# A two-layer graph-attention kernel: the last product of layer 1 is moved directly behind its gather, and the rest of a step is put around it

## The chip, the cores and the metric

The kernel runs on one core of a Trainium2 chip. A core has five engines that run side by side and wait for each other through semaphores: TensorE (PE, the matrix products and transposes; its weight loads are listed apart as PEld), VectorE (DVE), ScalarE (ACT), GpSimd (POOL), and SyncE (SP), which here only issues transfers. TensorE writes to PSUM, a small memory[...]; everything that leaves PSUM is read by VectorE or ScalarE. The metric is the device time of one launch in microseconds. All arithmetic that matters here is in float32.

## The reference, cut to what is computed

There are 32 graphs (batches) of 512 nodes with 512 features, one 512x512 adjacency matrix, and two layers. Each layer is a layer norm, a ReLU, and an attention over the graph, added to its input.

```python
# layer 0: 8 heads of 64, masked softmax attention
h = relu(layernorm(x))
q, k, v = h @ Wq + bq, h @ Wk + bk, h @ Wv + bv          # split into heads
scores = q k^T / 8 + (1 - adj) * -1e9
x = x + (softmax(scores) v) @ Wo + bo
# layer 1: one head, additive attention
h = relu(layernorm(x))
hw = h @ W
e = leaky_relu(s1[:, None] + s2[None, :], 0.2) * adj      # s1, s2: hw times two vectors
x = x + elu(softmax(e) @ hw + beta * hw)
```

## The kernel before: the parts that the change touches

The kernel works on several batches at once. In step `b` it does the attention of layer 0 for batch `b` in four units (one for each pair of heads), the product with Wo for batch `b-1`, layer 1 for batch `b-2`, and the norm, transposes and projections k and q for batch `b+1`. A string gives the order of the parts on TensorE. Digits are units, a dot is the denominators of the unit just finished:

```python
        order = {
            0: "0.V1.NH2c.3wK.Q", 1: "0.VUrR1.W2.NH3K.Q", B - 1: "0.VDU1.rRGX2.W3.t", B: "0yrR.zUWDngY",
            B + 1: "DgJY",
        }.get(b, "0.VDU1.GX2.rYNRWH3.KQ")
```

So in the steps 2 to 30: V is the projection to v, D the small product for layer 1's denominators, U the combinations for Wo, G the gather of layer 1 (`at` times `hn`, four tiles), X the combinations of its result gT, r and R load the two pairs of residual rows, Y is the final product of layer 1, N the transposes of the next batch, W the product with Wo, H the combinations of the transposed rows, K and Q the projections.

Each 512x512x512 product is done in seven half-size block products instead of eight. The seven pieces share three PSUM buffers, x, y and qz[...], and take sums and differences of blocks ("combinations") of the one side, which GpSimd forms:

```python
    def seven(name, w, B, tokens, one, two, scale=1.0, more=None):
        ...
        times(x_, A11, "b11", True);  nc.scalar.copy(y_, x_);            yield
        times(qz[:, 0, :], S1, "t1", True); nc.scalar.activation(q_, qz[:, 0, :], AF.Copy, scale=scale)
        if more: more(q_)                                                # yield
        times(y_, S2, "t2", False, onto=True); nc.scalar.copy(z_, y_);   yield   # z_ is qz[:, 1, :]
        times(x_, A12, "b21", False, onto=True); one(0, 0, x_);          yield
        times(z_, S3, "t3", False, onto=True);   two(1, 1, z_, q_);      yield
        times(y_, S4, "b22", False, onto=True);  two(0, 1, y_, q_);      yield
        times(z_, NA22, "t4", False, onto=True); one(1, 0, z_)
```

(Put on fewer lines here; the kernel has one statement on each.) `one` and `two` empty a finished block. For the final product of layer 1 that is the ELU, in turns on ScalarE and VectorE, and then an addition on GpSimd and the store; y is a pool of three buffers:

```python
        def elu(i, k, s):
            y = wtile([P, N], f"y_{b}_{i}_{k}", "y", 3)
            for t in range(2):
                nc.scalar.activation(y[:, ts(t, H)], s[:, ts(t, H)], AF.Exp, scale=r[...])
            nc.vector.tensor_scalar(y, y, 1.0, -1.0, op0=ALU.min, op1=ALU.add)
            for t in range(2):
                nc.vector.scalar_tensor_tensor(y[:, ts(t, H)], s[:, ts(t, H)], r[...], y[:, ts(t, H)],
                                               op0=ALU.mult, op1=ALU.max)
            ... # GpSimd adds the residual rows, SyncE stores
        def two(i, k, p, q):
            s = wtile([P, N], f"yq_{b}_{i}_{k}", "y", 3)
            nc.vector.tensor_tensor(s, p, q, op=ALU.add)
            elu(i, k, s)
```

A unit first multiplies the exponentials of the unit before with v (`values`, into the PSUM buffer po), then makes four score products into the buffers s, x and y, qz, s. VectorE masks each, ScalarE takes the exponential, VectorE sums the four (es):

```python
            for k, tag in enumerate(("s", "xy", "qz", "s")):
                scores(b, j, k, s, tag)
```

The transposes, sixteen for a batch, go through po, qz and s, and ScalarE empties them with the ReLU:

```python
        def second():
            for c, tag in ((2, "po"), (3, "qz")):
                ...
                turned(p, c)
                nc.scalar.activation(h[1][:, c - 2, :], p, AF.Relu)
        def first():
            p = psum.tile([P, 2, N], F32, name=f"pn0_{b}", tag="s")
            ...
            nc.scalar.activation(h[0], p, AF.Relu)
        for part in (second, first) if b else (first, second):
            part()
```

The combinations of gT: X makes them after the whole gather, with the first one in place; a second form, used by the last steps only, takes the first combination from the first two of the four tiles, into a buffer of its own:

```python
        def X():
            old["gB"] = combos(b - 2, "vT", old["g"])
        def G1():
            G((0, 1))
            t1 = first_combo(b - 2, "vT", old["g"][0], nc.gpsimd)
            G((2, 3))
            old["gB"] = other_combos(b - 2, "vT", old["g"], t1)
        def W():
            need("wa")
            fourth(b - 1, "uT", prev["oT"])      # the fourth combination, GpSimd
            run(out_proj(b - 1, prev))
```

Every engine works through its instructions in the order in which the program records them. For work that can stand anywhere on VectorE (sums, reciprocals, norms) the program keeps a rough clock of its own while it is built, and `GAP` is the allowed delay of two kinds of them, the sums and the reciprocals, for the four units; so the tuple only orders VectorE's instructions.

Of the kernel before, what the change touches and what calls it, by code (L numbers as in the profile page):

```python
# [40 lines left out]

A11, A12, NA22, S1, S2, S3, S4 = range(7)

GAP = (12.0, 14.0, 28.0, 24.0)
GAPS = {0: (14.0, 1.0, 4.0, 24.0), 1: (12.0, 12.0, 2.0, 14.0)}
LAST_GAPS = (3.0, 14.0, 12.0, 3.0)

# [16 lines left out]
def kernel(  # L64
# [86 lines left out]
    def wtile(shape, name, tag, bufs, dt=F32):  # L151
        return work.tile(shape, dt, name=name, tag=tag, bufs=bufs)
# [12 lines left out]
    def pe(us):  # L165

        clock["pe"] += us
        till = clock["pe"] + (1.0 if at_ends[0] else 0.4)
        while True:
            due = [i for i, (_, t, _) in enumerate(ends) if t <= till]  # L170
            fits = [
                (by, i) for i, (_, t, cost, _, by) in enumerate(spare)
                if max(clock["dve"], t) + cost <= till
            ]
            if due:
                ends.pop(due[0])[2]()
            elif fits:
                run_spare(min(fits)[1])
            else:
                return  # L180

    def dve(us):

        clock["dve"] = max(clock["dve"], clock["pe"]) + us
# [10 lines left out]
    def need(key):  # L195

        waits = at_ends[0] and key not in ("e", "es") and any(e[0] == key for e in spare + ends)
        run_all(key)
        if waits:
            clock["pe"] = max(clock["pe"], clock["dve"])  # L200
# [165 lines left out]
    def pair(b, name, p, tag, bufs):  # L366
        return wtile([P, 2, N], f"{name}_{b}_{p}", tag, bufs)
# [15 lines left out]
    def first_combo(b, name, pair0, eng):  # L383

        t1 = wtile([P, 2, H], f"{name}1_{b}", "T", 5)
        eng.tensor_tensor(t1, pair0[:, :, H:], pair0[:, :, :H], op=ALU.subtract)
        return t1
# [8 lines left out]
    def fourth(b, name, B):  # L396

        B["t4"] = wtile([P, 2, H], f"{name}4_{b}", "T", 5)
        nc.gpsimd.tensor_tensor(B["t4"], B["t2"], B["b21"], op=ALU.subtract)

    def turn(b, st):

        xs = st["x"]
        need(("x", b))
        h = [pair(b, "hT", i, "hP", 2) for i in range(2)]

        def turned(p, c):
            for t in range(T):
                nc.tensor.transpose(p[:, ts(t, P)], xs[t][:, ts(c, P)], ident)  # L409

        def second():
            for c, tag in ((2, "po"), (3, "qz")):
                p = psum.tile([P, 1 if c == 2 else 2, N], F32, name=f"pn{c}_{b}", tag=tag)[:, 0, :]
# [5 lines that stand above are left out]
            for c in range(2):  # L419
                turned(p[:, c, :], c)  # L420
            nc.scalar.activation(h[0], p, AF.Relu)

        for part in (second, first) if b else (first, second):
            part()
        pe(2.4)
        st["h"] = h

# [94 lines left out]
    def quarter(p):  # L522
        return p.rearrange("p (t f) -> p t f", t=2)

    def proj_v(b, st):
        v = st["v"] = [pair(b, "v", i, "vP", 2) for i in range(2)]

        def one(i, k, p):
            nc.scalar.copy(v[k][:, :, ts(i, H)], quarter(p))

        def two(i, k, p, r):
            nc.vector.tensor_tensor(v[k][:, :, ts(i, H)], quarter(p), quarter(r), op=ALU.add)
            dve(0.75)

        return seven(f"v{b}", wv, st["hT"], True, one, two)
# [7 lines left out]
    def gap(b, j):  # L543
        return (LAST_GAPS if b == B - 1 else GAPS.get(b, GAP))[j]

# [115 lines left out]
    def out_proj(b, st):  # L661
        x1 = st["x1"]
        st["mv"] = wtile([P, T, 2], f"mv1_{b}", "mv1", 2)
        st["s12"] = wtile([P, 2, T], f"s12_{b}", "s12", 2)
        st["hn"] = [None] * T

        def parts(k, i, p):

            n = 2 // len(x1[k])
            for u, r in enumerate(x1[k]):  # L670
                yield r[:, :, ts(i, H)], quarter(p)[:, u * n : (u + 1) * n, :]

        def add(i, k, p):
            for r, p_ in parts(k, i, p):
                nc.vector.scalar_tensor_tensor(r, p_, 1.0 / VS, r, op0=ALU.mult, op1=ALU.add)  # L675
                dve(0.75 if len(x1[k]) == 1 else 0.45)

        def one(i, k, p):
            add(i, k, p)
            if i == 1:  # L680
                norm1(b, st, (0, 1))

        def two(i, k, p, r):
            add(i, k, p)
            if i == 0:
                norm1(b, st, (2, 3))

        def more(q_):
            for i in (1, 0):
                for r, q in parts(1, i, q_):  # L690
                    nc.gpsimd.tensor_tensor(r, r, q, op=ALU.add)

        return seven(f"w{b}", wo, st["oT"], True, one, two, 1.0 / VS, more)
# [168 lines left out]
    def denominators(b, j):  # L862
        done = (b, j - 1) if j else (b - 1, NP - 1)
        if done[0] in states:
            finish(*done, states[done[0]])

    def step(b):

        cur, nxt = states.get(b), states.get(b + 1)
        prev, old = states.get(b - 1), states.get(b - 2)

        def run(pieces):
            for _ in pieces:
                pass

        def V():
            run(proj_v(b, cur))

        def G(cs=range(C)):
            for c in cs:
                gather(b - 2, c, old)

        def y_(g):
            st = states[g]
            st["pieces"] = final(g, st)
            for _ in range(3):
                next(st["pieces"])

            B = st["gB"]
            B["t4"] = B["t2"]
            nc.gpsimd.tensor_tensor(B["t4"], B["t2"], B["b21"], op=ALU.subtract)

        def z_(g):
            run(states[g]["pieces"])

        def Y():
            y_(b - 2)
            z_(b - 2)  # L900
# [11 lines that stand above are left out]
        def turned():  # L912
            turn(b + 1, nxt)
            if b + 2 < B:
                new_state(b + 2)

        def W():
            need("wa")
            fourth(b - 1, "uT", prev["oT"])
            run(out_proj(b - 1, prev))  # L920


        def H_():
            nxt["hT"] = combos(b + 1, "tT", nxt["h"])

        def K():
            fourth(b + 1, "tT", nxt["hT"])
            run(proj_k(b + 1, nxt))

        def U():  # L930
            need("rd")
            if b == B:
                prev["oT"] = other_combos(b - 1, "uT", prev["o"], prev["t1"])
            else:
                prev["oT"] = combos(b - 1, "uT", prev["o"])

        def T1():
            cur["t1"] = first_combo(b, "uT", cur["o"][0], nc.gpsimd)

        parts = {  # L940
            "V": V, "D": lambda: diagonal(b - 2, old), "G": G, "Y": Y, "N": turned, "W": W,
            "y": lambda: y_(b - 3), "z": lambda: z_(b - 3), "X": X, "g": G1,
            "K": K, "U": U, "H": H_, "r": lambda: residual(b - 1, prev, 0, *(("e", 4) if b == B else ())),
            "t": T1, "n": lambda: run_all(("hn", b - 1)), "J": judge,
            "R": lambda: residual(b - 1, prev, 1, *{B: ("e", 4), B - 1: ("x", 4)}.get(b, ())),
            "Q": lambda: run(proj_q(b + 1, nxt)),
            "c": lambda: value_row(ao, bvr), "w": row_constants,
        }
        order = {
            0: "0.V1.NH2c.3wK.Q", 1: "0.VUrR1.W2.NH3K.Q", B - 1: "0.VDU1.rRGX2.W3.t", B: "0yrR.zUWDngY",  # L950
            B + 1: "DgJY",
        }.get(b, "0.VDU1.GX2.rYNRWH3.KQ")
        unit_ = 0
        at_ends[0] = b < 2 or b >= B - 1
        for part in order:
            if part.isdigit():
                unit_ = int(part)
                unit(b, unit_)
            elif part == ".":
                denominators(b, unit_)  # L960
            else:
                parts[part]()
        states.pop(b - 3, None)
# [18 lines left out]
    with tc.manual_schedule(engines=BY_HAND):  # L982
# [9 lines left out]
        y_ = psum.tile([P, N], F32, name="y_first", tag="y")  # L992
# [231 lines left out]
```

## Time and profile before

The median of three runs is 3856.84 us (3854.91 to 3858.11). The profiled execution spans 3855.6 us.

| engine | busy us | share of the span | instructions |
|---|---|---|---|
| TensorE, products | 3622.9 | 94% | 25845 |
| TensorE, weight loads | 2025.5 | 53% | 25846 |
| VectorE | 2830.3 | 73% | 4335 |
| ScalarE | 1477.2 | 38% | 2310 |
| GpSimd | 1291.1 | 33% | 1090 |

The transfers move 120.82 MB at 31 GB/s on average. The mean granted clock of TensorE is 0.971 of full speed. The products are pipelined and their ends are modelled, so a busy TensorE is not one at its peak: where one piece follows the other, the distance from start to start is the time to count, not the duration. A line of the profile may be that of a helper (L53 is `product`), so the names of the tiles tell the parts apart: `x_y`, `qz_y` and `y_y` are the final product of layer 1, those with `_w` the product with Wo, `pg` the gather, `pn` the transposes, `po` the values, `ps` the scores.

### The profile page before, as it was taken

Reading aid. Unit: us, or ns where it says so; the run is one execution under the profiler, and the core shown is the slowest. Engines: PE = TensorE matmul, PEld = TensorE weight load, DVE = VectorE, ACT = ScalarE, POOL = GpSimd, SP = SyncE. Lnnn points to the kernel's source line nnn. Section 1 sums busy time; section 2 is a strip of 40 time slices with the busy share of each in tenths; the row PEclk is TensorE's granted clock in tenths of the full one; section 3 lists DMA queues with packets and bytes.
Section 4 is the critical chain, followed back from the end, with each engine's and each line's share of the span. In section 5 each row is a group of like instructions: output and inputs, shape, how many; then the busy total and the mean of one; then the engine's idle time right before and its main releaser. Section 6 shows DMA issues by size and latency. Waiting matters only on the chain. (4 is left out here: it accounts for less than half of the span.)

```text
span 3855.6 us, 62638 instructions
## 1 busy us (share of the span) xinstructions
PE 3622.9 (94%) x25845; PEld 2025.5 (53%) x25846; DVE 2830.3 (73%) x4335; ACT 1477.2 (38%) x2310; POOL 1291.1 (33%) x1090
## 2 busy tenths in 40 slices
PE   9999999999999999999999999999999999999986
PEld 5555555555554555555555545555455555555543
DVE  7978777787677776777876778767777767787774
ACT  3433343343333333343434334333433333343432
POOL 5432333322343232333223342324332333322341
PEclk9999999999999999999999999999999999999998
DMA  3010111100111001111011110111110111101100
GB/s 124 17 36 4 37 36 36 34 7 33 37 36 33 24 16 36 36 34 36 4 37 36 36 34 9 31 36 36 34 36 4 36 36 36 34 4 37 31 25 26
DMA packets 88035, 120.82 MB, mean 31 GB/s; under 512 B 11904, under 2 KB 49792, under 8 KB 87744
## 3 DMA queue, kind: packets, MB, share of 16 engines
q1 hardware_dynamic: 86160, 114.91, 9.5%
q8 instruction: 205, 3.36, 0.4%
q10 hardware_dynamic: 1376, 1.57, 0.1%
q14 instruction: 86, 0.70, 0.1%
q0 software_dynamic: 208, 0.27, 0.0%
HBM read 83.11 MB, written 33.62 MB: 30 GB/s over the span
## 5 line engine op out<-in xcount | busy, mean ns | idle before, releaser
L634 POOL TENSOR_TENSOR oT<-oT,rd 128x512 f32<-128x512 f32 x128 | 170.4, 1331 | 1622.4 <-ACT rd L633 1622.2
L582 ACT ACTIVATE e<-e 128x1024 f32<-128x1024 f32 x512 | 541.1, 1057 | 192.1 <-DVE e L567 157.7
L567 DVE SCALAR_TENSOR_TENSOR e<-maskT,ps 128x1024 f32<-128x1024 uint8 x384 | 454.7, 1212 | 145.2 <-PE ps L555 145.0
L555 PE MATMUL ps<-qT,kT 64*128 64x512 f32 x2048 | 483.4, 606 | 12.4 <-DVE e L567 12.4
L605 PE MATMUL po<-e,v 128*64 128x512 f32 x2048 | 463.0, 593 | 0.0
L53 PE MATMUL pg<-at,hn 128*64 128x512 f32 x2048 | 448.6, 596 | 4.2 <-DVE dmax L788 2.1
L628 DVE RECIPROCAL rd<-pd 128x256 f32<-128x256 f32 x256 | 434.9, 1729 | 1.2 <-POOL oT L634 1.2
L579 DVE TENSOR_TENSOR es<-es,e 128x1024 f32<-128x1024 f32 x254 | 342.1, 1347 | 16.9 <-ACT e L582 1.1
L555 PEld LDWEIGHTS ps<-qT,kT 64*128 64x128 f32 x2048 | 184.2, 186 | 309.1 <-issue 213.9
L53 PEld LDWEIGHTS pg<-at,hn 128*64 128x64 f32 x2048 | 148.5, 138 | 297.8 <-issue 289.3
L605 PEld LDWEIGHTS po<-e,v 128*64 128x64 f32 x2048 | 157.0, 138 | 235.9 <-issue 226.1
L409 PE MATMUL pn<-ident,x 128*128 128x128 f32 x512 | 106.4, 379 | 162.1 <-DVE y L816 161.7
L824 POOL TENSOR_TENSOR y<-y,x 128x512 f32<-128x512 f32 x124 | 157.2, 1268 | 245.0 <-DVE y L816 204.5
L613 ACT COPY oT<-po 128x512 f32<-128x512 f32 x128 | 73.8, 576 | 397.5 <-PE po L605 397.5
L675 DVE SCALAR_TENSOR_TENSOR x<-x_w,x 128x512 f32<-128x512 f32 x32 | 22.1, 690 | 274.1 <-issue 262.0
L729 DVE CUSTOM_DVE_ANT_0 scr<-hn,wa_r 128x512 f32<-128x512 f32 x256 | 168.0, 712 | 49.0 <-ACT hn L716 49.0
L756 ACT ACTIVATE at<-at 128x512 f32<-128x512 f32 x128 | 80.4, 628 | 274.4 <-DVE at L752 274.4
L633 ACT ACTIVATE rd<-rd 128x512 f32<-128x512 f32 x128 | 80.7, 630 | 272.6 <-DVE rd L628 272.5
L334 POOL TENSOR_TENSOR rs<-rs,mhalf 128x2 f32<-128x2 f32 (+1 forms) x97 | 77.9, 803 | 317.5 <-DVE rs L333 313.9
L409 PEld LDWEIGHTS pn<-ident,x 128*128 128x128 f32 x512 | 87.5, 198 | 181.6 <-issue 180.7
L654 POOL TENSOR_TENSOR x<-x,c_row 128x512 f32<-128x512 f32 x124 | 158.2, 1298 | 52.4 <-DMA x<-in_x_dram 52.4
L814 DVE TENSOR_SCALAR y<-y 128x512 f32<-128x512 f32 x128 | 61.5, 481 | 153.2 <-ACT y L811 153.2
(221 smaller groups left out, 6796.9 us busy)
## 6 DMA issues: line engine op xcount, KB each, us to landing
x<-in_x_dram SPq DMA_DIRECT2D x128, 256.0 KB, 4.7
out_dram<-y SPq DMA_DIRECT2D x128, 256.0 KB, 2.1
x<-in_x_dram SPq DMA_DIRECT2D x63, 512.0 KB, 4.0
s<-row_s SPq DMA_DIRECT2D x32, 256.0 KB, 4.0
adj<-in_adj_dram SPq DMA_DIRECT2D x4, 256.0 KB, 7.0
wk<-in_L_gnn_Wk_dram ACTq DMA_DIRECT2D x3, 256.0 KB, 9.5
wq<-in_L_gnn_Wq_dram SPq DMA_DIRECT2D x3, 256.0 KB, 7.1
wv<-in_L_gnn_Wv_dram SPq DMA_DIRECT2D x3, 256.0 KB, 5.3
```

Of the source, the lines that this page charges most:

```text
L53: nc.tensor.matmul(out[s : s + HD], lhsT[:, s : s + HD], rhs, start=start, stop=stop, skip_group_check=onto)
L409: nc.tensor.transpose(p[:, ts(t, P)], xs[t][:, ts(c, P)], ident)
L555: nc.tensor.matmul(ps[s], st["kT"][j][rows, ts(k, P)], st["qT"][j][rows, :], start=True, stop=True)
L567: nc.vector.scalar_tensor_tensor(e, maskT[:, k, :].unsqueeze(1).to_broadcast([P, 2, N]), NEG, p, op0=ALU.mult, op1=ALU.add)
L579: (nc.gpsimd if early else nc.vector).tensor_tensor(es, one, e, op=ALU.add)
L582: nc.scalar.activation(e, e, AF.Exp)
L605: nc.tensor.matmul(po[s * HD : (s + 1) * HD, :], v[k // 2][:, k % 2, (2 * j + s) * HD : (2 * j + s + 1) * HD], e[k][:, s, :], start=k == 0 ...
L628: nc.vector.reciprocal(rd[:, ts(k, H)], pd[:, ts(k, H)])
L634: nc.gpsimd.tensor_tensor(o, o, rd, op=ALU.mult)
L654: eng.tensor_tensor(r[:, t, :], r[:, t, :], c_row, op=ALU.add)
L729: nc.vector.tensor_tensor_reduce(scr, st["hn"][t], r, 1.0, 0.0, op0=ALU.mult, op1=ALU.add, accum_out=st["s12"][:, g, t : t + 1],)
L824: (nc.vector if b == B - 2 else nc.gpsimd).tensor_tensor(yu, yu, x_[:, :, ts(i, H)], op=ALU.add)
```

## The change

The order of the steps 2 to 30 becomes: final product of layer 1 directly behind its gather (with the first combination from half the gather), then unit 2, then the product with Wo, the transposes, unit 3, k and q. In the new part M the fourth combination for Wo is formed after the third piece, so that it may take the place of the second combination, which is then used up. The transposes go through s first, then po and qz. The tuple `GAP` is set to the new order. No operation on numbers is added or removed. It is meant to put other work between a product and the next use of the PSUM buffers that it leaves full.

```diff
-GAP = (12.0, 14.0, 28.0, 24.0)
+GAP = (13.0, 26.0, 14.0, 24.0)
...
-        for part in (second, first) if b else (first, second):
-            part()
+        first()
+        second()
...
+        def M():
+            pieces = out_proj(b - 1, prev)
+            for _ in range(3):
+                next(pieces)
+            fourth(b - 1, "uT", prev["oT"])
+            run(pieces)
+
...
-            "K": K, ... "X": X, "g": G1,
+            "K": K, ... "X": X, "M": M, "g": G1,
...
-        }.get(b, "0.VDU1.GX2.rYNRWH3.KQ")
+        }.get(b, "0.VDU1.rgY2.RMNH3.KQ")
```

(The table of parts is cut: M is added to it, and nothing else in it changes.)

More of the change, by code (lines that the diff above doesn't have):

```diff
@@ L941, in step @@
             "V": V, "D": lambda: diagonal(b - 2, old), "G": G, "Y": Y, "N": turned, "W": W,
-            "y": lambda: y_(b - 3), "z": lambda: z_(b - 3), "X": X, "g": G1,
+            "y": lambda: y_(b - 3), "z": lambda: z_(b - 3), "X": X, "M": M, "g": G1,
             "K": K, "U": U, "H": H_, "r": lambda: residual(b - 1, prev, 0, *(("e", 4) if b == B else ())),
```

## The prediction, made before the changed kernel ran

> **What bounds the kernel now.** I read the page's first part, then TensorE's list of waits, then one steady step on each engine. The page gives TensorE 3622.9 us of busy time in a span of 3855.6 us (94%), VectorE 73%, ScalarE 38%, GpSimd 33%. The page's chain of the work that ended last covers only the tail (1% of the span), so it is no help here. The waits of TensorE are (engine, line, releaser: total us, times, longest):
>
> ```profile
> PE pn L409 <- DVE y L816: 161.7, 29, 6.5
> PE pe L53 <- DVE as L763: 19.1, 2, 11.7
> PE ps L555 <- DVE e L567: 12.4, 33, 1.7
> PE qz_w L53 <- DVE y L816: 5.5, 1, 5.5
> PE pd L620 <- DVE rd L628: 3.9, 1, 3.9
> ```
>
> One wait stands out: 29 times, once in each of the steps 2 to 30 that the change rewrites, the transposes of the next batch wait 161.7 / 29 = 5.58 us for the end of the ELU of layer 1. The others lie in the first and last steps, except the 0.33 us of the scores in each step. The timeline of TensorE in such a step (start, duration, engine and line, operation):
>
> ```profile
> 1811.06 1.90 PE L53 MATMUL qz_y<-w,vT 128*64 128x256 f32 x16
> 1812.88 0.66 PE L409 MATMUL pn<-ident,x 128*128 128x128 f32 x4
> 1819.05 2.80 PE L409 MATMUL pn<-ident,x 128*128 128x128 f32 x12 [5.51 <-DVE y L816]
> 1821.77 3.47 PE L53 MATMUL x_w<-wo,oT 128*64 128x256 f32 x16
> 1825.07 1.89 PE L53 MATMUL qz_w<-wo,oT 128*64 128x256 f32 x16
> ...
> 1911.62 3.60 PE L605 MATMUL po<-e,v 128*64 128x512 f32 x16
> 1915.15 3.71 PE L555 MATMUL ps<-qT,kT 64*128 64x512 f32 x16
> 1918.78 1.08 PE L620 MATMUL pd<-es,ones 128*64 128x512 f32 x4
> ```
>
> The reader is to see three things. The seventh piece of the final product starts at 1811.06; a piece takes 1.73 us from start to start, so the product is over for TensorE at 1812.79, which I call E below. The second transposed column, which goes into the PSUM buffer qz, cannot start before 1819.05, which is E + 6.26. And a unit of attention (values, four score products, denominators) takes 1919.69 - 1911.62 = 8.07 us, in which the third score product, again into qz, starts 3.53 + 2 x 0.9 = 5.33 us after the unit's start.
>
> The wait costs more than its length. The stretches of clock (stretch, length, busy times of the five engines, granted clock, DMA):
>
> ```profile
> 1815.00:1819.00 4.00, 0.00 (x0) 0.00 (x0) 2.82 (x7) 1.32 (x3) 1.26 (x1) 0.88 0.30 107
> 1819.00:1822.00 3.00, 2.95 (x14) 2.65 (x16) 1.56 (x1) 0.72 (x2) 1.32 (x2) 0.50 0.87 291
> 1822.00:1825.00 3.00, 3.00 (x16) 1.68 (x16) 0.00 (x0) 0.90 (x1) 3.00 (x3) 0.52 1.02 278
> 1825.00:1828.00 3.00, 3.00 (x32) 1.95 (x28) 0.00 (x0) 1.80 (x4) 2.09 (x3) 1.00 0.70 253
> ```
>
> After the idle time the clock is at half for some 6 us, and the twelve transposes take 2.72 us (1819.05 to 1821.77). In the first batch, at full clock and without a wait, sixteen take 1.80 us, as this line shows (1.97 less a tail of 0.17), so twelve would take 1.35:
>
> ```profile
> 14.11 1.97 PE L409 MATMUL pn<-ident,x 128*128 128x128 f32 x16
> ```
>
> That is 1.37 us lost. The first piece of Wo (x_w) loses too: its group is busy for 149.9 us, the like group x_y for 121.5; 28.4 / 29 = 0.98 us in each step. Together 2.35 us.
>
> [...] the waits of 5.5 us are followed by half clock, the one of 3.87 us (near 128 us) too, with 0.57 in the stretch after it, while a wait of 1.69 us at 79 us leaves the clock at 1.00. [...] the three sums es take 4.98 us (1899.22 to 1904.20) beside GpSimd's combinations and 3.80 us alone, so small slacks must not be trusted.
>
> **The change part by part.** No arithmetic is added or removed: products, evictions and combinations are the same in number. What moves:
>
> *1. The final product no longer stands ahead of the transposes, but of unit 2.* Removed: 5.58 + 2.35 = 7.93 us per step. A step now takes (3596.96 - 279.40) / 28 = 118.49 us, from the waits at these two times; TensorE alone would need 110.56. As a check, by starts in the step: five products of seven pieces 35 x 1.727 = 60.4, four units 33.0, gather 13.7, the small product pe 1.0, transposes 1.8: 109.9.
>
> *2. The new wait behind it.* The chain of the last ELU stays as it is: VectorE and ScalarE go to and fro through four blocks, some 3.1 us each, and the ending is at E + 6.26. In front of the first need of qz now stand the values and three score products, 5.33 us. Wait: 6.26 - 5.33 = 0.93 us. VectorE then masks the first score, 1.2 us, to E + 7.45, and the fourth score product needs that buffer at E + 7.16 (6.26 + 0.9): 0.3 us more. Sum 1.2 us.
>
> *3. The final product directly behind the gather.* Its second piece needs the first combination of gT. That is why it now comes from half the gather: it can start after the second of four columns, some 6 us early. Its third piece needs the second combination, 3.45 us after the gather's end at 1911.62, so at 1915.07. The last eviction ends at 1912.42. But the new GpSimd order puts the root of the next batch's variance ahead, and VectorE has sums (to 1904.2), reciprocals (3.36) and statistics (3.3, by the trace of before) ahead of that: 1910.9, root at 1912.1. Then 1.28 us of combination: 1913.7. In time by 1.3 us; counted as 0.
>
> *4. Wo behind unit 2.* It starts at E + 8.07 + 1.2 = E + 9.3. Its residual rows were requested at 1818.13 and there at 1821.95, E + 9.2; their additions (2.5), those of the piece q (2.5, not before E + 13.4) and the fourth combination (1.3) end at E + 17.2. The seventh piece needs it at E + 9.3 + 6 x 1.727 = 19.7. On VectorE masks (4.6), sums (3.8) and half a reciprocal (1.7) end at E + 16.4, the fourth piece at 16.2. No wait.
>
> *5. Transposes behind Wo, in the new order s, po, qz.* qz is free when VectorE has added Wo's last piece, 0.9 us after the product's end; qz comes third, at 0.92 + 0.45 = 1.37. No wait. But the values of unit 3 follow at 1.82 and need po. ScalarE empties s first: it starts at about 1.15, takes 1.02 (the 128x1024 form), then po 0.6: about 2.65. Wait: 0.8 us.
>
> *6. k and q, unit 0, V.* Same order as before, on TensorE and about it; the small waits stay in the 110.56.
>
> New step: 110.56 + 1.2 + 0.8 = 112.56 us, 5.93 less. 29 x 5.93 = 172 us. 3856.84 - 172 = 3685 us. The first two and last three steps keep their order but for the transposes of two batches; I count them as 0, and put 3 us on for them.
>
> **The rivals.**
>
> *A. The wait only moves and keeps its size.* VectorE is busy for 73%, and in unit 2 it must now finish the ELU, mask four scores and sum them with little between. For it: the ELU chain is the same length, and TensorE now reaches x, y, qz and s all within 8 us. Against it: before, VectorE stood idle for 9.97 us ahead of Wo's first addition and had sums and reciprocals beside the ELU; the new order fills that hole. If 4 us of wait remain but the clock holds, the saving is 3.9 x 29 = 114 us: 3743 us. [...]
>
> *B. GpSimd's combination becomes the bound behind the gather.* Slack of 1.3 us, and the sums on VectorE are stretched while GpSimd works. Each us late costs 29 us: at 1.5 us of wait, 3728 us.
>
> *C. No new waits at all.* If the ELU chain tightens by 1 us, now that no other sums stand in the queue, and po is empty in time, all of 7.93 x 29 = 230 us is won: 3627 us. Against it: in the trace of before the chain was held by ScalarE's and VectorE's own exchange, not by those sums.
>
> **Range and chances.** I predict 3688 us. The removed 7.93 us are read from the trace in 29 like steps and are sure to 0.3 us. The new waits of 2.0 us may be 0.5 to 3.7 per step: 3688 - 44 = 3644, 3688 + 49 = 3737. The 2% mark is at 3780 us, for which the new waits would have to be over 5 us in a step; 0.92 for faster, 0.06 within 2%, 0.02 slower.
>
> **What would show it.** Right: the wait of pn for y is gone; TensorE's list has in its place some 0.9 us per step of ps for y L816 and some 0.8 us of po for hT; the clock is at 1.00 in the middle of the span; steps of about 112.6 us. Part 3 is wrong if y_y waits for vT. Part 4 is wrong if qz_w waits for uT or if VectorE's additions come late for the transposes. The prediction as a whole falls if [...] TensorE's pieces take longer than 1.73 us with the denser order.

## The result, and the profile after

The changed kernel takes 3696.21 us (median; 3695.18 to 3697.75), the kernel before 3856.70 us. The ratio is 0.9584, with a 95% interval of 0.9568 to 0.9601: 160 us less. The prediction said 3688 us.

TensorE's waits in the changed kernel (engine, line, tile, releaser: total us, times, longest):

```profile
PE ps L555 <- DVE y L816: 29.6, 29, 2.0
PE po L605 <- ACT hT L415: 22.6, 31, 0.8
PE pe L53 <- DVE as L763: 19.1, 2, 11.7
PE ps L555 <- DVE e L567: 11.6, 31, 1.1
PE y_k L53 <- ACT y_k L450: 6.3, 30, 0.3
```

The 161.7 us of pn for y are gone. The two new waits are the scores that wait for the end of the ELU, 29.6 / 29 = 1.02 us a step, and the values that wait for the transposes' eviction, 0.73 us. The third new line, y_k, is hardly a new wait: it is 0.20 us in a step and was 0.11 us before, which the list leaves out. The waits in the first and last steps (pe) are as before. TensorE's timeline in one step, from the last piece of the final product on:

```profile
1733.60 1.90 PE L53 MATMUL qz_y<-w,vT 128*64 128x256 f32 x16
1735.33 3.60 PE L605 MATMUL po<-e,v 128*64 128x512 f32 x16
1738.86 1.99 PE L555 MATMUL ps<-qT,kT 64*128 64x512 f32 x8
1741.60 2.17 PE L555 MATMUL ps<-qT,kT 64*128 64x512 f32 x8 [0.75 <-DVE y L816]
1743.69 1.08 PE L620 MATMUL pd<-es,ones 128*64 128x512 f32 x4
1744.60 1.90 PE L53 MATMUL x_w<-wo,oT 128*64 128x256 f32 x16
...
1756.79 1.97 PE L409 MATMUL pn<-ident,x 128*128 128x128 f32 x16
1759.48 3.65 PE L605 MATMUL po<-e,v 128*64 128x512 f32 x16 [0.73 <-ACT hT L415]
```

E, the end of the final product on TensorE, is 1735.33 here. The third score product starts at 1741.60 = E + 6.27, as the transposes did before; only now 5.33 us of other work stand ahead. The four score products take 4.83 us from 1738.86 to 1743.69, where they took 3.63 before: 1.20 us. And x_w follows with 1.73 us to the next piece, without the slow start. The clock (the column ahead of the last two) over the place where it was at half before:

```profile
1739.00:1742.00 3.00, 2.25 (x10) 0.88 (x12) 2.07 (x4) 1.27 (x3) 1.60 (x2) 1.00 0.29 93
1742.00:1745.00 3.00, 3.00 (x16) 0.93 (x14) 3.00 (x5) 2.17 (x3) 1.19 (x2) 1.00 0.80 270
```

From gather to gather most steps take 112.44 to 112.53 us. But not all: eight of the 29 take 112.94 to 115.39 us, and the mean is 112.83. Before, the mean was 118.44 (by the same gathers). 29 x (118.44 - 112.83) = 163 us, which is the whole difference of the spans (3855.6 - 3693.4 = 162.2).

### The profile page after: what moved, and what is told of

The parts are those of the page before. It is cut to its first block, busy times and chain, and to the rows that moved or that the text cites. A ratio compares the mean times of both kernels' runs of the same rounds, so it can differ in the third digit from the quotient of the medians.

```text
span 3693.4 us, 62550 instructions
## 1 busy us (share of the span) xinstructions
PE 3568.2 (97%) x25845; PEld 1977.7 (54%) x25846; DVE 2948.4 (80%) x4335; ACT 1460.8 (40%) x2310; POOL 1392.8 (38%) x1090
## 5 line engine op out<-in xcount | busy, mean ns | idle before, releaser
L555 PE MATMUL ps<-qT,kT 64*128 64x512 f32 x2048 | 497.4, 613 | 41.2 <-DVE y L816 29.6
L579 DVE TENSOR_TENSOR es<-es,e 128x1024 f32<-128x1024 f32 x254 | 396.6, 1562 | 18.5 <-ACT e L582 1.6
L605 PEld LDWEIGHTS po<-e,v 128*64 128x64 f32 x2048 | 149.1, 138 | 253.5 <-issue 214.2
L654 POOL TENSOR_TENSOR x<-x,c_row 128x512 f32<-128x512 f32 x124 | 221.7, 1809 | 52.1 <-DMA x<-in_x_dram 52.1
L579 DVE TENSOR_TENSOR es<-e,e 128x1024 f32<-128x1024 f32 x127 | 189.9, 1495 | 1.5 <-PE pd L620 1.5
L53 PE MATMUL qz_y<-w,vT 128*64 128x256 f32 x1520 | 180.3, 379 | 2.0 <-DVE yq L836 2.0
L562 DVE SCALAR_TENSOR_TENSOR e<-maskT,ps 128x512 f32<-128x512 uint8 x256 | 163.4, 680 | 0.0
L802 ACT COPY gT<-pg 128x512 f32<-128x512 f32 x128 | 74.3, 581 | 213.6 <-PE pg L53 213.6
```

The costliest lines, as they stand in the source:

```text
L53: nc.tensor.matmul(out[s : s + HD], lhsT[:, s : s + HD], rhs, start=start, stop=stop, skip_group_check=onto)
L555: nc.tensor.matmul(ps[s], st["kT"][j][rows, ts(k, P)], st["qT"][j][rows, :], start=True, stop=True)
L562: nc.vector.scalar_tensor_tensor(e[:, s, :], maskT[:, k, :], NEG, ps[s], op0=ALU.mult, op1=ALU.add)
L579: (nc.gpsimd if early else nc.vector).tensor_tensor(es, one, e, op=ALU.add)
L605: nc.tensor.matmul(po[s * HD : (s + 1) * HD, :], v[k // 2][:, k % 2, (2 * j + s) * HD : (2 * j + s + 1) * HD], e[k][:, s, :], start=k == 0 ...
L654: eng.tensor_tensor(r[:, t, :], r[:, t, :], c_row, op=ALU.add)
```

## The experiments

Each is compared with the kernel before on the same chip. "Step" is the distance from one gather to the next.

### Useless work in the wait, of the kernel before

The edit puts products of constants into po, ahead of the transposes that overwrite it. It adds work and takes none away.

```diff
                 p = psum.tile([P, 1 if c == 2 else 2, N], F32, name=f"pn{c}_{b}", tag=tag)[:, 0, :]
+                if c == 2 and 3 <= b < B:
+                    for _ in range(24):
+                        product(nc, p[:, :H], ones, wq[:, A11, 0, :])
                 turned(p, c)
```

> Kernel before, with 24 useless pairs of products (some 0.216 us each, 5.2 us in all) put into the 5.58 us in which TensorE waits for the ELU, in each of 29 steps. Theory (the wait cost its own length and, apart from it, 2.35 us of half clock): the wait stays, filled, but the clock stays at 1.00, the twelve transposes take some 1.35 us instead of 2.72 and the first piece of Wo 1.73; 29 x 2.35 = 68 us less than before, some 3789 us, by more work. Rival (the slow transposes and the slow first piece have another cause, such as the loads of x that run at the same time): the time stays at 3857 us or rises.

Measured: 3925.94 us, ratio 1.0182 (1.0165 to 1.0199). The time went up, against the expectation, because I had sized the filling wrongly by a factor of two: a pair takes 0.436 us, not 0.216, and the filling overran the wait. TensorE's timeline in that kernel:

```profile
1844.72 10.53 PE L53 MATMUL pn<-wq,ones 128*64 128x256 f32 x96
1855.18 1.97 PE L409 MATMUL pn<-ident,x 128*128 128x128 f32 x16
1857.08 1.95 PE L53 MATMUL x_w<-wo,oT 128*64 128x256 f32 x16
1858.86 1.90 PE L53 MATMUL qz_w<-wo,oT 128*64 128x256 f32 x16
```

The theory's own signs are there: sixteen transposes in 1.90 us, where twelve took 2.72, and x_w 1.78 us to the next piece, where it took 3.30. All steps are equal at 120.8 us. Less the filling (1844.72 to 1855.18, 10.46 us) that leaves 110.37 us as TensorE's own work in a step, which the prediction had put at 110.56. So half clock cost 118.44 - 5.58 - 110.37 = 2.49 us a step.

### Half of it

The same edit with `range(12)`.

> As the first experiment, with half the useless products: there a pair took 0.436 us and the filling 10.46 us, twice what was meant. Twelve calls take 5.23 us and stay within the wait of 5.58. Theory (half clock is a loss of its own): the clock stays at 1.00, the rest of the wait is some 0.3 us; TensorE's own 110.37 us of a step, found in the first experiment as 120.83 - 10.46, and 5.9 of filling and waiting make 116.3 us a step, 29 x 2.1 = 62 us less than before: some 3794 us. Rival (only the wait counts): 3856 us.

Measured: 3801.60 us, ratio 0.9861 (0.9844 to 0.9877), step mostly 116.18, mean 116.48. Adding 5.2 us of useless work to each step made the kernel before 54 us faster. The rival is out: the wait of 5.58 us had a second price. The 8 us that miss from the expectation lie in irregular steps (up to 118.33 us); in eight of the 29 ScalarE waits 2.7 us or more for a store (4.41 us in that one); the experiment with yq below takes this up.

### The transposes through po, s, qz

```diff
-        first()
-        second()
+        column(2, "po")      # the body of second(), for one column
+        first()
+        column(3, "qz")
```

> Changed kernel, but the transposes go to po first, then s, then qz. Theory (the values of unit 3 wait 0.8 us because po is emptied behind the long eviction of s): the wait of po for hT goes, qz is third and not needed sooner than before, 31 x 0.73 = 23 us less than 3696: some 3673 us. Rival (the wait moves to the combinations of hT or to the scores of unit 3, which need s): 3690 us or more.

Measured: 3673.44 us, ratio 0.9525 (0.9509 to 0.9541), 22.8 us less than the changed kernel. The wait of po is not in the list any more, and no other took its place: the common step is 111.66, down by 0.80.

### The sums yq in buffers of their own

`yq` is written to the four buffers of the gather's operand `at`, which are free by then, in place of the ELU's three.

```diff
-            s = wtile([P, N], f"yq_{b}_{i}_{k}", "y", 3)
+            s = wtile([P, N], f"yq_{b}_{i}_{k}", *(("at", 4) if b < B - 3 else ("y", 3)))
```

> Changed kernel, but the sums q + p of the final product (yq) take buffers that the gather has just freed, not the pool of three of the ELU. Theory (the end of the ELU chain, 6.27 us behind the product, is set by these buffers: the third block waits for the store of the first, the fourth for the third's last VectorE operation): the fourth exponential starts some 1.6 us sooner, the chain ends at about 4.7 us, before qz is needed at 5.33; the waits of ps for y (29.6 us, and the 0.2 us behind each) go, and so do the steps that are 0.6 to 3 us longer than 112.45: 35 + 11 = 46 us less, some 3650 us. Rival (the chain is set by the exchange of the two engines alone): 3690 us or more.

Measured: 3658.44 us, ratio 0.9489 (0.9473 to 0.9504), 38 us less than the changed kernel. What held the chain is seen in ScalarE's timeline of one of the long steps of the changed kernel:

```profile
376.24 0.91 ACT L811 ACTIVATE y<-yq,rd 128x256 f32<-128x256 f32 x2 [2.08 <-DVE yq L836]
380.61 0.91 ACT L811 ACTIVATE y<-yq,rd 128x256 f32<-128x256 f32 x2 [3.47 <-DMA out_dram<-y]
383.12 0.84 ACT L811 ACTIVATE y<-qz_y,rd 128x256 f32<-128x256 f32 x2 [1.60 <-PE ps L555]
```

The third exponential waits for a store: the buffer still holds the first block. The fourth stands idle for 1.6 us although its product is long done; the profile names TensorE's scores as its releaser, which came at about that time, but VectorE's last reading of the third block (382.07 to 382.95) is what frees its buffer. With the edit, the same operations in ScalarE's timeline:

```profile
1714.02 0.91 ACT L811 ACTIVATE y<-yq,rd 128x256 f32<-128x256 f32 x2 [2.08 <-DVE yq L836]
1716.94 0.91 ACT L811 ACTIVATE y<-yq,rd 128x256 f32<-128x256 f32 x2 [2.01 <-DVE yq L836]
1717.76 0.81 ACT L811 ACTIVATE y<-qz_y,rd 128x256 f32<-128x256 f32 x2
```

The fourth follows the third without a pause. The chain ends at 1720.55 on VectorE, 4.5 us behind the product's end (1716.06), ahead of the 5.33 at which qz is needed. The wait of the scores for y falls from 29.6 to 0.8 us, and nearly all steps take 111.46 to 111.50, none more than 112.11. The saving is 8 us smaller than I expected, but both parts of it, the wait and the irregular steps, are gone.

### Both edits

> The two edits together. Theory (the two waits are independent, on different buffers): the savings add, 23 + 46 = 69 us less than 3696, some 3627 us, with steps of 110.6 us, the time of TensorE's own work. Rival (without them VectorE, busy for 80%, sets the pace): less than two thirds of the sum, 3650 us or more, and a new wait for VectorE in TensorE's list.

Measured: 3635.23 us, ratio 0.9427 (0.9411 to 0.9443), 61 us less than the changed kernel, where the two alone gave 22.8 and 37.8, together 60.6. They add. The step is 110.68 in all but a few, 0.3 us above TensorE's own work, and of TensorE's waits in the steps 2 to 30 these two are all that is left to speak of:

```profile
PE ps L555 <- DVE e L567: 12.2, 32, 1.3
PE y_k L53 <- ACT y_k L450: 6.3, 30, 0.5
```

VectorE is no bound here, though it is busy for four fifths of the time. This is the shortest time of all versions here.

### All combinations of gT after the gather

```diff
-        }.get(b, "0.VDU1.rgY2.RMNH3.KQ")
+        }.get(b, "0.VDU1.rGXY2.RMNH3.KQ")
```

> Changed kernel, but the combinations of gT are all formed after the whole gather, as before the change. Theory (the final product can stand directly behind the gather only because its first combination comes from half of it): GpSimd is free at 0.3 us after the product's start at the soonest and has t3 (1.46) and t1 (1.28) to do before the second piece, due at 1.73: a wait of some 1.7 to 2.2 us for tT or vT in each of 29 steps, 50 to 64 us more than 3696, some 3750 us, and up to 40 more where such a wait lets the clock fall. Rival (GpSimd's combinations hide beside the first piece): 3696 us.

Measured: 3793.11 us, ratio 0.9834 (0.9818 to 0.9851), 97 us more than the changed kernel. TensorE's timeline:

```profile
1768.80 1.90 PE L53 MATMUL x_y<-w,gT 128*64 128x256 f32 x16
1772.78 3.59 PE L53 MATMUL qz_y<-w,gT 128*64 128x256 f32 x16 [2.09 <-POOL gT L379]
1776.21 1.90 PE L53 MATMUL y_y<-w,vT 128*64 128x256 f32 x16
...
1889.18 1.95 PE L53 MATMUL qz_y<-w,gT 128*64 128x256 f32 x16 [2.08 <-POOL gT L379]
```

The wait is there with the expected size, 60.3 us in 29 steps; the piece behind it takes 3.43 us to the next one instead of 1.73. That is half clock again (the mean granted clock is 0.983, in the changed kernel 0.991): behind 19 of the 28 waits of 2.08 to 2.10 us the piece lasts 2.58 us or more, behind the other nine 1.95, as in the next step (the last line). So three fifths of what the change gained hang on taking the first combination from half the gather.

### The old tuple in the new order

```diff
-GAP = (13.0, 26.0, 14.0, 24.0)
+GAP = (12.0, 14.0, 28.0, 24.0)
```

> Changed kernel with the tuple GAP of before. It moves one half of one reciprocal per step on VectorE by a few instructions, into a stretch with 1.5 us of idle time ahead of the masks of unit 3. Theory (the order on TensorE is what brings the time): 3696 us, within 4. Rival (the order on VectorE carries part of the gain): over 3705 us.

Measured: 3770.13 us, ratio 0.9777 (0.9761 to 0.9793), 74 us more than the changed kernel. My expectation failed. Most steps take 112.36 us, no more than in the changed kernel, but ten in a row (the eighth to the seventeenth) take 119.5 to 122.9. In them TensorE waits at the denominators of unit 3:

```profile
1718.19 3.71 PE L555 MATMUL ps<-qT,kT 64*128 64x512 f32 x16
1727.37 1.98 PE L620 MATMUL pd<-es,ones 128*64 128x512 f32 x4 [5.48 <-DVE rd L628]
1729.13 3.11 PE L53 MATMUL x_v<-wv,hT 128*64 128x256 f32 x16
```

and VectorE's timeline shows why:

```profile
1704.51 0.75 DVE L749 SCALAR_TENSOR_TENSOR at<-s,s,adjT 128x512 f32<-128x512 f32 x1
...
1721.70 2.34 DVE L567 SCALAR_TENSOR_TENSOR e<-maskT,ps 128x1024 f32<-128x1024 uint8 x2
1723.96 3.36 DVE L628 RECIPROCAL rd<-pd 128x256 f32<-128x256 f32 x2
```

The reciprocals of unit 2 read the one buffer pd. In these ten steps the program's own clock, by which it places such work while it is built, put layer 1's `at` and the masks of the next unit ahead of them, and pd stays full for 5.5 us too long. VectorE has this order in all ten steps; in the other 19 the reciprocals stand ahead of that work. My expectation rested on the order in one step, which is not one of the ten. Why the program's clock gives another order in just these ten is not shown.

### The old order of the transposes

> Changed kernel with the transposes in the old order po, qz, s. Theory (each of these waits is for one named buffer): qz is now due 0.45 us after the product with Wo and free at 0.9, so pn waits some 0.35 to 0.45 us for VectorE's last addition, and the wait of 0.73 us of po goes: 29 x 0.3 = 10 us less than 3696, some 3686 us. Rival (the order of before was part of the loss): 3700 us or more.

The edit puts `for part in (second, first) if b else (first, second): part()` back. Measured: 3684.90 us, ratio 0.9555 (0.9539 to 0.9571), 11 us less than the changed kernel; the wait of po is gone, and pn waits 6.2 us in 29 steps for VectorE's last addition to Wo, 0.21 us each. This part of the change cost time.

### The yq buffers in the old order

> Kernel before, in its old order, with the yq sums in buffers that the gather has freed (the one edit of the third experiment). Theory (the ELU chain shortens by 1.4 us from its own buffers, whatever stands behind the product, but 4 us of wait stay if the transposes come next): the wait of pn for y falls from 5.58 to some 4.1 us, the clock still drops in each step; 29 x 1.45 = 42 us less than 3856: some 3814 us. Rival (the order is not needed, shorter buffers' waits do it all): under 3720 us.

Measured: 3789.36 us, ratio 0.9829 (0.9813 to 0.9846), 66 us less than before. The wait of pn for y is 112.7 / 29 = 3.89 us, so the chain is shorter by 1.69 us. Beyond that, half clock costs less; the mean granted clock is 0.980, before it was 0.971. From the start of the transposes behind the wait to Wo's second piece TensorE takes 4.55 to 4.85 us in all 29 steps. Before, it took 5.05 to 6.14 us in the 20 steps with 6.8 us of half clock, and 4.55 to 4.64 us in the nine with 3.4. The cost is now 116.08 (the mean step) - 3.89 - 110.37 = 1.82 us instead of 2.49, which is why the step is 2.4 us shorter and not 1.7. Neither theory is right to the end: the buffers alone bring two fifths of the change's gain, but the transposes still wait.

### The new tuple in the old order

> Kernel before, in its old order, with the new tuple GAP alone. The tuple was worth 74 us in the new order, where it kept one reciprocal ahead of layer 1's work in ten steps. Theory (the tuple has no gain of its own, it must fit the order): it moves the sums of unit 1 behind the statistics, all within VectorE's idle time of before; the wait of pn for y stays at 5.58 us: 3856 us, within 8. Rival (the tuple carries a large part of the change's gain by itself): under 3815 us.

Measured: 3858.84 us, ratio 1.0010 (1.0001 to 1.0018); pn waits for y for 162.0 us in 29 steps, as before. The tuple has no gain of its own.

## Why the prediction was right, point by point

**Part 1, what is removed.** Right, and shown. The 5.58 us of wait went. Half clock as a second price was read from the trace at 2.35 us a step; with the wait filled it comes out at 2.49.

**Part 2, the wait behind the final product.** Right where the step is undisturbed: 0.93 + 0.3 was expected, 1.20 measured in the step shown. The ending of the ELU stays at E + 6.27. The reason that I gave was incomplete: I took the chain for an exchange of two engines, 3.1 us a block, but the experiment with yq in buffers of its own shows that 1.6 us of its end are a wait for a buffer. And one term was left out: eight steps are longer, the worst by 3 us (part of it half clock), because the third block waits for a store. They are exactly the eight of the 29 in which ScalarE waits for out_dram, 2.87 to 3.54 us each; the store of the first block takes 2.9 to 3.6 us to land there, where the median of all stores is 2.3. With buffers of its own for yq these steps are gone but for two of 0.6 us. Without that the mean would be at the common 112.45, so it is (112.83 - 112.45) x 29 = 11 us, somewhat more than the 8 us between the prediction and the result. The kernel before had only two such waits in its 29 steps (3.21 and 2.96 us), and the prediction has no term for them; why the stores take longer in some steps the runs do not show.

That the expected 112.56 lies so close to the common 112.45 is partly luck: TensorE's own work was put 0.19 us too high (110.56, measured 110.37), and small waits of 0.15 us (112.45 - 110.37 - 1.20 - 0.73), of which y_k is 0.09, were left out.

**Part 3, the combination.** Right: y_y waits for nothing. The slack was 0.9 us instead of 1.3 (the second combination ends at 1725.77, the third piece starts at 1726.69), because the sums on VectorE took 5.87 us beside GpSimd's work instead of 4.98, and the root behind them, not the last eviction, came last. The experiment with the late combinations shows what a miss here costs: 97 us, of which 60 are the wait.

**Part 4, Wo.** Right that TensorE doesn't wait; the fourth combination ends at 1754.19, the seventh piece starts at 1754.96: 0.8 us of slack, not 2.5. That this combination stands behind the third piece (part M) was not tried on its own, so its share is not shown. VectorE's first addition starts at E + 18.1, not at 16.4. These are the lines of VectorE's sums, before and after:

```profile
L579 DVE TENSOR_TENSOR es<-es,e 128x1024 f32<-128x1024 f32 x254 | 342.1, 1347 | 16.9 <-ACT e L582 1.1 <-DVE es L579 0.5
```

```profile
L579 DVE TENSOR_TENSOR es<-es,e 128x1024 f32<-128x1024 f32 x254 | 396.6, 1562 | 18.5 <-ACT e L582 1.6 <-DVE es L579 0.5
```

The mean grows from 1347 to 1562 ns, and GpSimd's additions of c_row from 1298 to 1809 ns: the new order lays these sums and additions side by side (a sum that starts at 1745.95 takes 2.33 us, while c_row is added until 1747.19; the median of such sums is 1.22). Why they take longer there is not shown. I had said not to trust small slacks; this one held by 0.8 us.

**Part 5, the transposes.** Right: 0.8 us expected, 0.73 measured, and removed by changing the order.

**Part 6, the rest of the step is unchanged.** Right for this kernel, but the reason given in the front of the document and carried into the sum, that the tuple only orders VectorE's instructions and so counts for nothing, hides 74 us. The new tuple doesn't bring a gain; it averts a loss that the new order would otherwise have in ten steps.

**The rivals.** A (the wait keeps its size) is out: 1.02 us is left of 5.58. B (GpSimd becomes the bound) is out for this kernel and true for the kernel with the late combinations. C (no new waits) did not come about by itself, but with two edits of buffers it does: its 3627 us stand against the 3635 measured.

**Which waits bring half clock.** The trace of before had half clock behind waits of 3.87 us and more, and none behind one of 1.69 us. The runs show that the length alone does not decide it. In the kernel with the late combinations 19 of the 28 waits of 2.08 to 2.10 us were followed by a slow piece and nine were not; behind a wait of 1.79 us two scores took 3.02 us to the denominators, behind one of 1.78 us 2.09. In the changed kernel the waits of 1.96 and 2.04 us (near 386 and 1515 us) were followed by 3.41 us of half clock, from 0.83 and 1.36 us behind their ends on, those of 1.91 and 2.02 us were not. These four differ in where they lie: in the traces of before and after the stretches of half clock (34 and 7) start whole multiples of 3.413 us apart, to 0.01 us, and if the changed kernel's time is laid off in such lengths from one of these starts, the waits of 1.96 and 2.04 us lie within one length, and those of 1.91 and 2.02 are divided, with 1.2 and 1.3 us in the longer part. Whether that is what decides was not shown. That the prediction's sum has no half clock behind such waits did no harm, because the new waits are mostly about 1 us; it would have, had rival A come at 2 us.

## What to carry to other kernels

When the busiest engine waits for a buffer, find the two moments that count, when it is freed and when it is next needed, and put as much other work between them as the gap is long; what remains is the difference, here to a tenth of a microsecond. Then ask what frees the buffer so late: here a pool of three, in which one block waited for VectorE's reading of the block before and another at times for a store, was worth 38 us more, with no change of order. And check every step of a schedule that the program places by a clock of its own: one steady step says nothing of ten others.

## What the runs showed of the hardware that I had not expected

A wait of about 2 us can have a second price nearly as high: behind 2.08 to 2.10 us of idle time TensorE's next piece was slow in 19 of 28 cases, and took up to 3.45 us instead of 1.78. Waits of equal length differ in this. Filling 5.2 of an idle 5.58 us with useless products made the kernel before 54 us faster. And the second price is not the same each time: behind the waits of mostly 5.5 us in the kernel before, half clock lasted 6.8 us in 20 of 29 steps and 3.4 us in the other nine. In the 20 it began 0.74 us or more ahead of the wait's end, in the nine 0.55 us at most. Behind the waits of mostly 3.87 us, with the yq buffers in the old order, the work behind the wait took 4.55 to 4.85 us in all 29 steps, about as long as in those nine (4.55 to 4.64).
